# Attention in four whole-pair units, s1 as a row through DRAM, and a new order of a step

## Chip, cores and metric

One core of one Trainium2 chip. The metric is device time in microseconds (us), the median over executions. The kernel before takes 3942.5 us (three runs) and 3941.88 us (3939.61 to 3942.74, four runs) beside the changed one.

## The reference

Two layers over 32 batches of 512 tokens with 512 features, all in 32-bit floats:

```
h  = relu(layernorm(x))
q, k, v = h@Wq + bq, h@Wk + bk, h@Wv + bv                # 8 heads of 64
attn = softmax(q k^T / 8 + (1 - adj) * -1e9)
x  = x + (attn @ v) @ Wo + bo
h  = relu(layernorm(x));   g = h@W
s1, s2 = g@a1, g@a2                                      # one number per token
e  = leaky_relu(s1[:, None] + s2[None, :], 0.2) * adj
x  = x + elu(softmax(e) @ g + beta * g)
```

## The kernel before

It is software-pipelined by hand: step b does V (the v product) and the attention of batch b, the graph part (diagonal, gathers, finals) of b-2, the out projection W of b-1, and the transposes, K and Q of b+1. V, W, K and Q are Strassen products in seven parts. The orders of TensorE and VectorE are fixed by the program text; `later(key, wait, cost, fn)` puts VectorE work `wait` us (of a model of time) later, and `need(key)` forces it out. ScalarE and GpSimd are ordered by a scheduler. Cut to what the argument touches:

```python
def values(b, j, st, half):          # half a pair of heads at a time
    ...
def finish(b, j, st):
    for n in range(b - 1, b + 1):
        need(("at", n))              # the masked exps that read the spread of s1 come first
    pd = psum.tile([P, N], F32, name=f"pd_{b}_{j}", tag="pd")
    ...                              # pd = sum of the exps, by TensorE
    nc.vector.reciprocal(rd, pd)

def logits(b, st):
    dg = row_diag(work, s12[:, 0, :], f"s1_{b}")         # VectorE: diagonal of s1
    def rest(k):
        z = wtile([P, N], f"at_{b}_{k}", "at", 4)
        nc.vector.scalar_tensor_tensor(z, st["ps1"], s12[:, 1, k:k+1], adjT[:, k, :], op0=ALU.add, op1=ALU.mult)
        nc.vector.scalar_tensor_tensor(z, z, ALPHA, z, op0=ALU.mult, op1=ALU.max)
        nc.scalar.activation(z, z, AF.Exp)
        ...                                              # GpSimd: as = sum of the four z
    def spread():
        st["ps1"] = row_bcast(psum, dg, f"s1_{b}")       # TensorE: ones x diagonal, into tag "pd"
        for k in range(T):
            later(("at", b), 0.3, 1.35, lambda k=k: rest(k))

def strassen(pieces, n=1, between=None, early=None):     # in step(b)
    for i, _ in enumerate(pieces):
        if i == 0: ...; att(n, ("qz", "s"))              # attention in 8 half units,
        if i == 4 and between: between()                 # also inside a product
```

Names in the traces: `x`, `y` and `qz` with v, w, k or q are the PSUM tiles in which the seven parts of that product are summed, one line for each part. `ps` are the scores, `e` their exps, `es` the sums of `e`, `po` the values and `pd` the softmax sums of a pair of heads. `oT` is `po` after the division; its sums and differences (the combinations) feed the product W. In the graph part `at` are the masked exps, `as` is their sum over the four tiles, `pe` its sum by TensorE (the diagonal, D in the order strings), `pg` are the gathers (G) and `py` the finals (Y). `hn` is the second normalisation, and the dots make s1 and s2 from it. `pn` are the transposes (N), `pbs` is the product that spreads s1, `dgs` its diagonal. A PSUM `tag` is a buffer that tiles of that tag use in turn.

## Time and profile before

| | before |
|---|---|
| span of the profiled run, mean granted clock of TensorE | 3938.1 us, 0.986 |
| V of batch 0 starts | 98.3 us |
| steps 0 and 1 | 81.2 + 101.8 us |
| a steady step (V to V, batches 2 to 31) | 118.18 us |
| from V of batch 31 to the end | 229.7 us |

TensorE is the bound; the prediction shows its lines. Here is the line of the steady steps of the kernel before (from:to, us, then busy time and count of PE, PEld, DVE, ACT and POOL, the granted clock, the DMA share and GB/s). The clock is 1.00: TensorE never slows in these steps.

```profile
281.30:3708.40 3427.10, 3301.40 (x21928) 1565.80 (x21926) 2155.68 (x3296) 1266.53 (x1917) 1962.58 (x1707) 1.00 0.08 27
```

In the tail it does. Behind a wait of 12.82 us pbs takes 1.97 us there and eight score products 3.74, where the prediction's lines of a steady step show 1.08 and 1.99:

```profile
3799.87 1.97 PE L46 MATMUL pbs<-dgs,ones 128*64 128x512 f32 x4 [12.82 <-DVE dgs L123]
3801.78 3.74 PE L446 MATMUL ps<-qT,kT 64*128 64x512 f32 x8
```

### The profile page before, as it was taken

To read this page: it belongs to the slowest core of one execution; us is meant where nothing else is said; L and a number is where in the kernel's file an instruction comes from. 1 tells how busy PE (TensorE), PEld (TensorE's weight loads), DVE (VectorE), ACT (ScalarE), POOL (GpSimd) and SP (SyncE) were. 2 spreads that over 40 slices of the span, in tenths; PEclk is the share of its full clock that TensorE was granted. 3 is DMA by queue.
4 is the path that set the end of the run, shared out by engine and by line. 5 is a ranking of instruction groups with operands and counts; after the bars stand their busy time and mean duration, and the time that the engine had idled before them with its cause. 6 is when DMAs were issued, how large, how long until landed. Compare 5 with 4: busy or idle time off the path is not lost.

```text
span 3938.1 us, 59207 instructions
## 1 busy us (share of the span) xinstructions
PE 3691.0 (94%) x24302; PEld 1752.0 (44%) x24302; DVE 2414.3 (61%) x3712; ACT 1400.7 (36%) x2119; POOL 2192.5 (56%) x1922
## 2 busy tenths in 40 slices
PE   5989999999999999999999999999999999999976
PEld 3444444444444444444444444444444444444422
DVE  4466566666566665566665566665566665566653
ACT  1333333333333333333333333333333333333321
POOL 4555555555655555655555655555655555655552
PEclk7999999999999999999999999999999999999988
DMA  3000000001100011000111000101100100000001
GB/s 105 11 12 33 33 27 7 33 33 33 33 21 13 33 33 33 33 24 10 33 33 33 33 22 12 33 33 33 33 18 16 33 33 33 33 19 15 22 22 33
DMA packets 60373, 111.61 MB, mean 28 GB/s; under 512 B 5632, under 2 KB 9728, under 8 KB 60096
## 3 DMA queue, kind: packets, MB, share of 16 engines
q1 hardware_dynamic: 54848, 101.73, 7.7%
q10 hardware_dynamic: 4880, 5.24, 0.4%
q8 instruction: 192, 3.15, 0.3%
q0 software_dynamic: 368, 0.79, 0.1%
q14 instruction: 85, 0.70, 0.1%
HBM read 74.19 MB, written 33.55 MB: 27 GB/s over the span
## 4 chain that ended last, share of the span: by engine, by line
PE 72%; DVE 14%; POOL 7%; issue 4%; ACT 3%; DMA 1%; POOLq 0%; ACTq 0%; DVEq 0%
PE pg L46 11%; PE ps L446 11%; PE po L471 9%; PE py L46 6%; PE qz_v L46 4%; PE qz_w L46 4%; POOL es L462 3%; PE pd L486 3%; DVE rd L495 3%; PE y_v L46 3%; PE x_v L46 3%; PE x_w L46 3%; PE qz_k L46 3%; DVE e L451 3%; PE qz_q L46 3%
## 5 line engine op out<-in xcount | busy, mean ns | idle before, releaser
L462 POOL TENSOR_TENSOR es<-es,e 128x512 f32<-128x512 f32 x512 | 645.8, 1292 | 622.1 <-ACT e L455 622.1
L451 DVE TENSOR_TENSOR e<-ps,nmT 128x1024 f32<-128x1024 f32 x512 | 604.3, 1217 | 612.1 <-PE ps L446 612.1
L455 ACT ACTIVATE e<-e 128x1024 f32<-128x1024 f32 x512 | 540.5, 1056 | 519.6 <-DVE e L451 505.1
L446 PE MATMUL ps<-qT,kT 64*128 64x512 f32 x2048 | 513.1, 620 | 0.6 <-POOL qT L402 0.6
L462 POOL TENSOR_TENSOR es<-e,e 128x512 f32<-128x512 f32 x256 | 325.9, 1294 | 334.5 <-PE pd L486 212.7
L471 PE MATMUL po<-e,v 128*64 128x512 f32 x2048 | 496.1, 605 | 0.8 <-ACT e L455 0.7
L495 DVE RECIPROCAL rd<-pd 128x512 f32<-128x512 f32 x128 | 429.8, 3358 | 91.3 <-PE pd L486 91.3
L46 PE MATMUL pg<-at,hn 128*64 128x512 f32 x2048 | 452.8, 595 | 9.5 <-DVE dmax L613 7.7
L46 PE MATMUL py<-w,gT 128*64 128x512 f32 x2048 | 450.0, 592 | 0.0
L446 PEld LDWEIGHTS ps<-qT,kT 64*128 64x128 f32 x2048 | 177.5, 187 | 278.6 <-issue 222.3
L46 PEld LDWEIGHTS pg<-at,hn 128*64 128x64 f32 x2048 | 148.3, 138 | 302.4 <-issue 302.1
L46 PEld LDWEIGHTS py<-w,gT 128*64 128x64 f32 x2048 | 147.6, 137 | 291.8 <-issue 291.8
L640 DVE TENSOR_SCALAR y<-y 128x512 f32<-128x512 f32 x128 | 84.1, 657 | 313.7 <-ACT y L639 313.7
L471 PEld LDWEIGHTS po<-e,v 128*64 128x64 f32 x2048 | 124.0, 136 | 342.2 <-issue 338.2
L267 POOL TENSOR_TENSOR rs<-rs,mhalf 128x1 f32<-128x1 f32 x256 | 168.5, 661 | 153.3 <-DVE rs L266 135.8
L643 POOL TENSOR_TENSOR y<-y,x 128x512 f32<-128x512 f32 x128 | 161.8, 1274 | 139.6 <-DVE y L641 139.6
L510 POOL TENSOR_TENSOR x<-x,c_row 128x512 f32<-128x512 f32 x128 | 162.4, 1290 | 131.3 <-DMA x<-in_x_dram 131.0
L486 PE MATMUL pd<-es,ones 128*64 128x512 f32 x512 | 141.8, 604 | 63.5 <-DVE at L575 55.9
L499 POOL TENSOR_TENSOR oT<-oT,rd 128x512 f32<-128x512 f32 x128 | 168.7, 1318 | 52.4 <-DVE rd L495 47.4
L639 ACT ACTIVATE y<-py,rd 128x512 f32<-128x512 f32 x128 | 87.4, 683 | 246.9 <-PE py L46 183.0
L498 ACT ACTIVATE rj<-rd 128x512 bf16<-128x512 f32 x128 | 80.6, 630 | 247.8 <-DVE rd L495 239.1
L626 ACT COPY gT<-pg 128x512 f32<-128x512 f32 x128 | 74.4, 581 | 260.9 <-PE pg L46 260.9
(190 smaller groups left out, 5694.3 us busy)
## 6 DMA issues: line engine op xcount, KB each, us to landing
x<-in_x_dram SPq DMA_DIRECT2D x128, 256.0 KB, 4.7
x<-in_x_dram SPq DMA_DIRECT2D x64, 512.0 KB, 4.0
out_dram<-y SPq DMA_DIRECT2D x128, 256.0 KB, 3.8
adj<-in_adj_dram SPq DMA_DIRECT2D x4, 256.0 KB, 7.6
w<-in_L_gnn_W_dram ACTq DMA_DIRECT2D x1, 1024.0 KB, 7.3
wk<-in_L_gnn_Wk_dram ACTq DMA_DIRECT2D x3, 256.0 KB, 5.0
wq<-in_L_gnn_Wq_dram ACTq DMA_DIRECT2D x3, 256.0 KB, 8.9
wv<-in_L_gnn_Wv_dram ACTq DMA_DIRECT2D x3, 256.0 KB, 6.5
```

Of the source, the lines that this page charges most:

```text
L46: nc.tensor.matmul(out[s : s + HD], lhsT[:, s : s + HD], rhs, start=start, stop=stop, skip_group_check=onto)
L267: nc.gpsimd.tensor_tensor(rstd, rstd, mhalf[:, 0:1], op=ALU.pow)
L446: nc.tensor.matmul(p[:, s, :], st["kT"][j][rows, ts(k, P)], st["qT"][j][rows, :], start=True, stop=True)
L451: nc.vector.tensor_tensor(e, p, nmT[:, k, :].unsqueeze(1).to_broadcast([P, 2, N]), op=ALU.add)
L455: nc.scalar.activation(e, e, AF.Exp)
L462: nc.gpsimd.tensor_tensor(es[:, s, :], one[:, s, :], e[:, s, :], op=ALU.add)
L471: nc.tensor.matmul(po[s * HD : (s + 1) * HD, :], v[k // 2][:, k % 2, (2 * j + s) * HD : (2 * j + s + 1) * HD], e[k][:, s, :], start=k == 0 ...
L486: nc.tensor.matmul(pd[s * HD : (s + 1) * HD, :], ones[:, :HD], st["es"][j][:, s, :], start=True, stop=True)
L495: nc.vector.reciprocal(rd, pd)
L499: nc.gpsimd.tensor_tensor(o, o, rd, op=ALU.mult)
L510: nc.gpsimd.tensor_tensor(r[:, t, :], r[:, t, :], c_row, op=ALU.add)
L643: nc.gpsimd.tensor_tensor(y, y, st["x1"][t // 2][:, t % 2, :], op=ALU.add)
```

## The change

The intent: attention in 4 units of a whole pair of heads between whole products (values and pd of the pair before, then four scores), so that TensorE goes half as often from 128-row products to the 64-row scores and back (a surplus of 0.35 us a visit in the trace before); s1 turned into a row by two DMAs through DRAM, so that pbs and the PSUM buffer shared with pd go; and an order of step, prologue and tail that has fewer waits.

```diff
-    def row_bcast(psum, dg, name): ...      # ones x diagonal on TensorE
+    def as_row(dst, col, name):
+        d = dram.tile([N], F32, name=f"row_{name}", tag="row")
+        nc.sync.dma_start(d.rearrange("(t p) -> p t", p=P), col, allow_slow_non_contiguous=True)
+        nc.sync.dma_start(dst, d.unsqueeze(0).to_broadcast([P, N]))
@@ attention
-    def values(b, j, st, half):
+    def values(b, j, st):                   # four k at once, then pd in the same tiling
-        for n in range(b - 1, b + 1):
-            need(("at", n))
@@ logits
-        dg = row_diag(work, s12[:, 0, :], f"s1_{b}")
+        as_row(row, s12[:, 0, :], f"s1_{b}")
-                later(("at", b), 0.3, 1.35, lambda k=k: rest(k))
+            later(("at", b), 5.0, 1.45, lambda k=k: rest(k))
@@ step                                      # digits are units of attention
+        order = {0: "0V1N2c3rKQ", 1: "0V1N2W3KQ", B - 1: "0VD1G2YW3", B: "0DGWY", B + 1: "DGY",
+        }.get(b, "0VD1G2YN3WKQ")
... (prologue: masks through four PSUM buffers, row constants moved into step 0; more T and oP buffers)
```

More of the change, by code (lines that the diff above doesn't have):

```diff
@@ L119 @@
     flag = ctile([1, 1], "flag", I32)
-    def row_diag(work, col, name):
-        dg = work.tile([P, T, P], F32, name="dg" + name, tag="dg", bufs=1)
-        nc.vector.tensor_tensor(
-            dg, ident.unsqueeze(1).to_broadcast([P, T, P]),
-            col.unsqueeze(2).to_broadcast([P, T, P]), op=ALU.mult,
-        )
-        return dg
-    def row_bcast(psum, dg, name):
-        p = psum.tile([P, N], F32, name="pb" + name, tag="pd")
-        product(nc, p, ones, dg.rearrange("p t n -> p (t n)"), start=True, stop=True)
-        return p
+    dram = ctx.enter_context(tc.tile_pool(name="dram", bufs=2, space=bass.MemoryType.DRAM))
+    def as_row(dst, col, name):
+        d = dram.tile([N], F32, name=f"row_{name}", tag="row")
+        nc.sync.dma_start(d.rearrange("(t p) -> p t", p=P), col, allow_slow_non_contiguous=True)
+        nc.sync.dma_start(dst, d.unsqueeze(0).to_broadcast([P, N]))
     nc.vector.memset(fin, 0.0)
@@ L192, in edges @@
             nc.vector.tensor_reduce(e0[:, t : t + 1], adj_sb[t], axis=AX.X, op=ALU.max)
-        nc.vector.tensor_scalar(e0, e0, 0.0, 1.0, op0=ALU.is_equal, op1=ALU.mult)
-        pe0 = row_bcast(psum, row_diag(work, e0, "e0"), "e0")
-        nc.vector.tensor_scalar(edge8, pe0, -(HD ** -0.5), HD ** -0.5, op0=ALU.mult, op1=ALU.add)
+        nc.vector.tensor_scalar(e0, e0, 0.0, HD ** -0.5, op0=ALU.not_equal, op1=ALU.mult)
+        as_row(edge8, e0, "e0")
     def masks():
-        for k in range(T):
-            p = psum.tile([P, N], F32, name=f"pa_{k}", tag="x")
+        for k, tag in enumerate(("x", "po", "pd", "s")):
+            p = psum.tile([P, N], F32, name=f"pa_{k}", tag=tag)
             for t in range(T):
@@ L202, in masks, with mask, other @@
             nc.scalar.copy(adjT[:, k, :], p)
+        def mask(k):
             m = wtile([P, N], f"m_{k}", "y", 3)
             nc.vector.tensor_scalar(m, edge8, -(HD ** 0.5), 1.0, op0=ALU.mult, op1=ALU.add)
-            nc.vector.tensor_tensor(m, p, m, op=ALU.max)
+            nc.vector.tensor_tensor(m, adjT[:, k, :], m, op=ALU.max)
             nc.vector.tensor_scalar(nmT[:, k, :], m, -NEG, NEG, op0=ALU.mult, op1=ALU.add)
-        for t in range(T):
+        def other(t):
             sq = wtile([P, N], f"sq_{t}", "y", 3)
@@ L213, in masks @@
             )
+        for k in range(T):
+            later("nm", 1.0, 1.9, lambda k=k: mask(k))
+        for t in range(T):
+            later("bad", 1.0, 1.4, lambda t=t: other(t))
     def load_blocks(w, ap, name):
@@ L244, in value_row, with dot @@
         nc.vector.tensor_add(c_row, c_row, p)
+        combine(nc.gpsimd, wo, ao)
     def row_constants():
         wa = wtile([P, 2, C], "wa", "wa", 1)
+        def dot(g, c, ar):
+            scr = wtile([P, D], f"scr_{g}_{c}", "y", 3)
+            nc.vector.tensor_tensor_reduce(
+                scr, w1[:, c, :], ar, 1.0, 0.0,
+                op0=ALU.mult, op1=ALU.add, accum_out=wa[:, g, c : c + 1],
+            )
+            if c == C - 1:
+                as_row((wa1_r, wa2_r)[g], wa[:, g, :], f"wa{g}")
         for g in range(2):
-            ar = wtile([P, D], f"a_{g}", "at", 4)
+            ar = wtile([P, D], f"a_{g}", "s1", 1)
             nc.gpsimd.dma_start(ar, bass.AP(tensor=a.tensor, offset=a.offset + g * D, ap=[[0, P], [1, D]]))
             for c in range(C):
-                scr = wtile([P, D], f"scr_{g}_{c}", "y", 3)
-                nc.vector.tensor_tensor_reduce(
-                    scr, w1[:, c, :], ar, 1.0, 0.0,
-                    op0=ALU.mult, op1=ALU.add, accum_out=wa[:, g, c : c + 1],
-                )
-        for g, dst in ((0, wa1_r), (1, wa2_r)):
-            p = row_bcast(psum, row_diag(work, wa[:, g, :], f"wa{g}"), f"wa{g}")
-            nc.scalar.copy(dst, p)
+                later("wa", 4.0, 0.75, lambda g=g, c=c, ar=ar: dot(g, c, ar))
     def stats(src, t, u, mv, rstd):
@@ L299, in block, with combos @@
         return pairs[i][:, :, ts(j, H)]
-    def combos(b, name, pairs, tag):
+    def combos(b, name, pairs):
         b11, b12, b21, b22 = (block(pairs, k) for k in range(4))
-        t2, t3, t4 = (wtile([P, 2, H], f"{name}{i}_{b}", tag, 3) for i in (2, 3, 4))
+        t2, t3, t4 = (wtile([P, 2, H], f"{name}{i}_{b}", "T", 5) for i in (2, 3, 4))
         nc.gpsimd.tensor_tensor(t3, b22, b12, op=ALU.subtract)
@@ L319, in turned @@
                 nc.tensor.transpose(p[:, ts(t, P)], xs[t][:, ts(c, P)], ident)
+        for c, tag in ((2, "po"), (3, "x")):
+            p = psum.tile([P, N], F32, name=f"pn{c}_{b}", tag=tag)
+            turned(p, c)
+            nc.scalar.activation(h[1][:, c - 2, :], p, AF.Relu)
         p = psum.tile([P, 2, N], F32, name=f"pn0_{b}", tag="s")
@@ L323, in turn @@
             turned(p[:, c, :], c)
-            nc.scalar.activation(h[0][:, c, :], p[:, c, :], AF.Relu)
-        p = psum.tile([P, N], F32, name=f"pn2_{b}", tag="x")
-        turned(p, 2)
-        nc.scalar.activation(h[1][:, 0, :], p, AF.Relu)
-        p = psum.tile([P, 2, N], F32, name=f"pn3_{b}", tag="qz")
-        turned(p[:, 0, :], 3)
-        nc.scalar.activation(h[1][:, 1, :], p[:, 0, :], AF.Relu)
-        pe(2.8)
-        st["hT"] = combos(b, "tT", h, "tT")
+        nc.scalar.activation(h[0], p, AF.Relu)
+        pe(2.4)
+        st["hT"] = combos(b, "tT", h)
     def seven(name, w, B, tokens, one, two):
@@ L406, in proj_k @@
     def proj_k(b, st):
-        kT = st["kT"] = [wtile([P, N], f"kT_{b}_{f}", "kT", 5) for f in range(C)]
+        kT = st["kT"] = [wtile([P, N], f"kT_{b}_{f}", "kT", 4) for f in range(C)]
         def one(i, k, p):
@@ L441, in scores @@
     def scores(b, j, k, st, tag):
-        p = psum.tile([P, 2, N], F32, name=f"ps_{b}_{j}_{k}", tag=tag)
+        if tag == "xy":
+            ps = [psum.tile([P, N], F32, name=f"ps{s}_{b}_{j}_{k}", tag=tag[s]) for s in range(2)]
+        else:
+            p = psum.tile([P, 2, N], F32, name=f"ps_{b}_{j}_{k}", tag=tag)
+            ps = [p[:, s, :] for s in range(2)]
         for s in range(2):
@@ L446, in scores @@
             nc.tensor.matmul(
-                p[:, s, :], st["kT"][j][rows, ts(k, P)], st["qT"][j][rows, :], start=True, stop=True
+                ps[s], st["kT"][j][rows, ts(k, P)], st["qT"][j][rows, :], start=True, stop=True
             )
-        pe(1.25)
+        pe(0.87)
         e = wtile([P, 2, N], f"e_{b}_{j}_{k}", "e", 4)
-        nc.vector.tensor_tensor(
-            e, p, nmT[:, k, :].unsqueeze(1).to_broadcast([P, 2, N]), op=ALU.add
-        )
-        dve(1.14)
+        if tag == "xy":
+            for s in range(2):
+                nc.vector.tensor_tensor(e[:, s, :], ps[s], nmT[:, k, :], op=ALU.add)
+            dve(1.38)
+        else:
+            nc.vector.tensor_tensor(
+                e, p, nmT[:, k, :].unsqueeze(1).to_broadcast([P, 2, N]), op=ALU.add
+            )
+            dve(1.2)
         nc.scalar.activation(e, e, AF.Exp)
@@ L462, in scores @@
                 nc.gpsimd.tensor_tensor(es[:, s, :], one[:, s, :], e[:, s, :], op=ALU.add)
-    def values(b, j, st, half):
-        if half == 0:
-            st["po"] = psum.tile([P, N], F32, name=f"po_{b}_{j}", tag="po")
-        po, e, v = st["po"], st["e"][j], st["v"]
-        for k in (0, 1) if half == 0 else (2, 3):
+    def values(b, j, st):
+        po = st["po"] = psum.tile([P, N], F32, name=f"po_{b}_{j}", tag="po")
+        e, v = st["e"][j], st["v"]
+        for k in range(T):
             for s in range(2):
@@ L475, in values @@
                 )
-        pe(1.72)
-        if half == 1:
-            finish(b, j, st)
-    def finish(b, j, st):
-        for n in range(b - 1, b + 1):
-            need(("at", n))
-        pd = psum.tile([P, N], F32, name=f"pd_{b}_{j}", tag="pd")
+        pd = st["pd"] = psum.tile([P, N], F32, name=f"pd_{b}_{j}", tag="pd")
         for s in range(2):
@@ L488, in finish @@
             )
-        pe(0.86)
+        pe(4.5)
         if j % 2 == 0:
-            st["o"].append(pair(b, "oT", j // 2, "oP", 3))
+            st["o"].append(pair(b, "oT", j // 2, "oP", 4))
+        nc.scalar.copy(st["o"][j // 2][:, j % 2, :], po)
+    def finish(b, j, st):
         o = st["o"][j // 2][:, j % 2, :]
-        nc.scalar.copy(o, st["po"])
         rd = wtile([P, N], f"rd_{b}_{j}", "rd", 1)
-        nc.vector.reciprocal(rd, pd)
+        nc.vector.reciprocal(rd, st["pd"])
         dve(3.3)
@@ L500, in finish, with residual @@
         if j == NP - 1:
-            st["oT"] = combos(b, "uT", st["o"], "uT")
-    def residual(b, st):
+            st["oT"] = combos(b, "uT", st["o"])
+    def residual(b, st, tag="x1", bufs=2):
         st["x1"] = []
         for i in range(2):
-            r = pair(b, "x1", i, "x1", 2)
+            r = pair(b, "x1", i, tag, bufs)
             nc.sync.dma_start(r, x[b, ts(i, H), :].rearrange("(t p) f -> p t f", p=P))
@@ L561, in third @@
             )
+            st["dots"] += 1
+            if st["dots"] == 2 * T:
+                logits(b, st)
         for t in rows:
@@ L566, in logits @@
     def logits(b, st):
-        need(("hn", b))
         s12 = st["s12"]
-        dg = row_diag(work, s12[:, 0, :], f"s1_{b}")
-        dve(0.65)
+        row = wtile([P, N], f"s1_{b}", "s1", 1)
+        as_row(row, s12[:, 0, :], f"s1_{b}")
         def rest(k):
@@ L575, in rest @@
             nc.vector.scalar_tensor_tensor(
-                z, st["ps1"], s12[:, 1, k : k + 1], adjT[:, k, :], op0=ALU.add, op1=ALU.mult
+                z, row, s12[:, 1, k : k + 1], adjT[:, k, :], op0=ALU.add, op1=ALU.mult
             )
@@ L585, in rest @@
                 nc.gpsimd.tensor_tensor(st["as"], st["as"], z, op=ALU.add)
-        def spread():
-            st["ps1"] = row_bcast(psum, dg, f"s1_{b}")
-            pe(0.86)
-            for k in range(T):
-                later(("at", b), 0.3, 1.35, lambda k=k: rest(k))
-        return spread
+        for k in range(T):
+            later(("at", b), 5.0, 1.45, lambda k=k: rest(k))
     def diagonal(b, st):
+        need(("hn", b))
         need(("at", b))
@@ L651, in new_state, with unit @@
             "x": load(b), "e": [[] for _ in range(NP)], "es": {}, "o": [], "at": [], "g": [], "gT": [],
+            "dots": 0,
         }
-    def unit(b, n, tags=("qz", "s")):
+        norm0(b, states[b]["x"])
+    def unit(b, j):
         s = states.get(b)
-        j, second = divmod(n, 2)
-        if s is not None:
-            for k in range(2):
-                scores(b, j, 2 * second + k, s, tags[k])
-        if second:
-            values(b, j, s, 0)
-        elif j:
-            values(b, j - 1, s, 1)
-        elif b - 1 in states:
-            values(b - 1, NP - 1, states[b - 1], 1)
+        done = (b, j - 1) if j else (b - 1, NP - 1)
+        if done[0] in states:
+            values(*done, states[done[0]])
+        if s is not None and j < NP:
+            for k, tag in enumerate(("s", "xy", "qz", "s")):
+                scores(b, j, k, s, tag)
+        if done[0] in states:
+            finish(*done, states[done[0]])
     def step(b):
@@ L674, in step @@
         prev, old = states.get(b - 1), states.get(b - 2)
-        todo = list(range(8)) if cur is not None else [0] if prev is not None else []
-        def att(n=1, tags=("s", "qz")):
-            for _ in range(n):
-                if todo:
-                    unit(b, todo.pop(0), tags)
-        def strassen(pieces, n=1, between=None, early=None):
-            for i, _ in enumerate(pieces):
-                if i == 0:
-                    if early:
-                        early()
-                    att(n, ("qz", "s"))
-                if i == 4 and between:
-                    between()
@@ L691, in step, with run, V, G @@
-        if cur is not None:
-            strassen(proj_v(b, cur), between=old and (lambda: diagonal(b - 2, old)))
-        else:
-            att()
-            if old is not None:
-                diagonal(b - 2, old)
-        if prev is not None:
-            residual(b - 1, prev)
-        att()
-        if old is not None:
+        def run(pieces):
+            for _ in pieces:
+                pass
+        def V():
+            run(proj_v(b, cur))
+        def G():
             for c in range(C):
-                if c == 2:
-                    att()
@@ L704, in step, with Y, turned @@
                 gather(b - 2, c, old)
-            att()
+        def Y():
             for t in range(T):
-                if t == 2:
-                    att()
                 final(b - 2, t, old)
-        elif cur is not None:
-            att()
-        if nxt is not None:
+        def turned():
             turn(b + 1, nxt)
-        if b == 0:
-            att(3)
-        if b == 1:
-            att(1)
-        if prev is not None:
-            strassen(out_proj(b - 1, prev))
-            if b == 1:
-                att(1)
@@ L722, in step, with W @@
-        if b + 2 < B:
-            new_state(b + 2)
-            norm0(b + 2, states[b + 2]["x"])
-        if nxt is not None:
-            strassen(proj_k(b + 1, nxt))
-        spread = logits(b - 1, prev) if prev is not None else None
-        if nxt is not None:
-            strassen(proj_q(b + 1, nxt), early=spread)
-        elif spread:
-            spread()
-        att(8)
-        if b == B:
+            if b + 2 < B:
+                new_state(b + 2)
+        def W():
+            residual(b - 1, prev, *(("e", 4) if b == B else ()))
+            run(out_proj(b - 1, prev))
@@ new lines, in step @@
+        parts = {
+            "V": V, "D": lambda: diagonal(b - 2, old), "G": G, "Y": Y, "N": turned, "W": W,
+            "K": lambda: run(proj_k(b + 1, nxt)), "Q": lambda: run(proj_q(b + 1, nxt)),
+            "c": lambda: value_row(ao), "r": row_constants,
+        }
+        order = {
+            0: "0V1N2c3rKQ", 1: "0V1N2W3KQ", B - 1: "0VD1G2YW3", B: "0DGWY", B + 1: "DGY",
+        }.get(b, "0VD1G2YN3WKQ")
+        for part in order:
+            if part.isdigit():
+                unit(b, int(part))
+            else:
+                parts[part]()
@@ L734, in step @@
+        if b == 0:
+            need("nm")
+            need("bad")
+        if b == B + 1:
             judge()
@@ L767 @@
                 product(nc, p[:, ts(t, P)], ones, ident, start=t == 0, stop=t == T - 1)
-        norm0(0, states[0]["x"])
+        need(("x", 0))
         combine(nc.vector, wk, ak)
@@ L774 @@
             pass
-        if B > 1:
-            new_state(1)
-            norm0(1, states[1]["x"])
+        new_state(1)
         masks()
+        combine(nc.gpsimd, wv, av, VS)
         for _ in proj_q(0, states[0]):
             pass
-        combine(nc.gpsimd, wv, av, VS)
-        value_row(ao)
-        combine(nc.gpsimd, wo, ao)
-        row_constants()
+        need("nm")
         for b in range(B + 2):
```

## The prediction

> **What bounds the kernel now.** I read the page's busy line first, then the waits of TensorE, then TensorE's instructions in order of time over one step, then GpSimd's over the same step.
>
> ```profile
> PE 3691.0 (94%) x24302; PEld 1752.0 (44%) x24302; DVE 2414.3 (61%) x3712; ACT 1400.7 (36%) x2119; POOL 2192.5 (56%) x1922
> PE pbs L46 <- DVE dgs L123: 59.0, 32, 12.8
> PE pd L486 <- DVE at L575: 55.9, 30, 4.4
> PE pn L319 <- ACT hT L324: 23.5, 32, 0.7
> PE qz_q L46 <- DVE qT L398: 12.3, 28, 0.4
> ```
>
> TensorE is the bound, 94% busy. Its waits are short but come once in every step (32 batches, so about 30 equal steps): the spread of s1 (pbs) waits for the diagonal product dgs, and pd waits for the at work that still reads pbs, because both share one PSUM buffer.
>
> ```profile
> 1565.95 1.08 PE L46 MATMUL pbs<-dgs,ones 128*64 128x512 f32 x4 [1.10 <-DVE dgs L123]
> 1579.88 1.95 PE L46 MATMUL qz_q<-tT,wq 128*64 128x256 f32 x16 [0.44 <-DVE qT L398]
> 1581.66 1.90 PE L46 MATMUL x_v<-wv,hT 128*64 128x256 f32 x16
> 1583.49 1.99 PE L446 MATMUL ps<-qT,kT 64*128 64x512 f32 x8
> 1585.40 1.94 PE L471 MATMUL po<-e,v 128*64 128x512 f32 x8
> 1589.12 1.08 PE L486 MATMUL pd<-es,ones 128*64 128x512 f32 x4 [1.78 <-DVE at L575]
> 1646.68 1.53 PE L319 MATMUL pn<-ident,x 128*128 128x128 f32 x12 [0.74 <-ACT hT L324]
> 1648.52 1.95 PE L46 MATMUL x_w<-wo,oT 128*64 128x256 f32 x16 [0.31 <-ACT hT L327]
> 1684.17 1.08 PE L46 MATMUL pbs<-dgs,ones 128*64 128x512 f32 x4 [1.10 <-DVE dgs L123]
> ```
>
> From pbs to pbs a step takes 1684.17 - 1565.95 = 118.22 us, of which 1.10 + 0.44 + 1.78 + 0.74 + 0.31 = 4.37 us is waiting and 1.0 us the pbs product. The starts also show what a change between kinds of product costs. One Strassen product takes 1.727 us from start to start (others of the row: 1570.64, 1572.37, 1574.09), but x_v to ps is 1.83, ps to po 1.91 and po to the next 1.77. In single instructions the surplus is 0.100 us ahead of ps, 0.104 after its first pair, 0.097 ahead of po and 0.051 after its first pair: 0.35 us for one visit, 8 visits a step, 2.8 us.
>
> GpSimd looks half idle, but its work comes in blocks:
>
> ```profile
> 1590.88 2.51 POOL L462 TENSOR_TENSOR es<-e,e 128x512 f32<-128x512 f32 x2
> 1593.34 1.28 POOL L585 TENSOR_TENSOR as<-as,at 128x512 f32<-128x512 f32 x1
> 1594.58 1.28 POOL L499 TENSOR_TENSOR oT<-oT,rd 128x512 f32<-128x512 f32 x1
> 1658.01 4.99 POOL L462 TENSOR_TENSOR es<-es,e 128x512 f32<-128x512 f32 x4
> ```
>
> Each 128x512 sum costs 1.25 us, and 1.35 when it depends on the one before.
>
> [...]a lone 256 KB store landed 2.0 us after its issue, a lone 512 KB load after 3.8.[...]
>
> **The change, part by part**, in a steady step, with those durations and the built program's order on each engine.
>
> 1. *Removed.* The pbs product and dgs (1.0 + 1.10), the wait of pd for at (1.78), of qz_q (0.44; kT and qT are now rewritten only after the last score), of pn and x_w (1.05; four PSUM buffers instead of three). All on TensorE's chain: 6.4 us.
> 2. *Fewer visits.* Values and the sum pd of the pair before now follow straight on a product of the same tiling, then four scores. Four visits instead of eight: 4 x 0.35 = 1.4 us saved.
>
> Unstalled, a step is then: 4 units of 3.44 (values) + 0.86 (pd) + 3.44 (scores) + 0.35 = 32.3; 28 Strassen products of 1.727 = 48.3; 8 gathers and finals of 3.485 = 27.9; transposes 1.95; diagonal sums 0.46. Sum 110.9 us, 7.3 below before.
>
> 3. *Added waits.* Take 0 for the start of a unit on TensorE. Scores begin at 4.4, e on VectorE starts at 5.6, 6.7, 8.0 and 9.1 (1.15 apart, the split one 1.25), reciprocal 10.3 to 13.6; the four exps end at 7.9, 9.1, 10.3 and 11.45; the product after the unit starts at 8.03.
>  - y copy: the product's third part needs x copied to y by ScalarE, which is behind the exps until 11.45 + 0.58 = 12.0, wanted at 11.5. 0.5 us, in V and in W: 1.0.
>  - Diagonal: on GpSimd the order is six es sums (from 9.15 to 16.65), oT (18.0), three combinations (22.0), and only then the last sum of as (23.4). TensorE reaches the diagonal after V at 20.7. Wait 2.8.
>  - K: after the finals GpSimd must take in the residual x1 by DMA (the load is issued only when y is done; 3.8 us each), the T combinations, then es, oT, T4, and only then the power for rs of the batch after next. Unit 3 starts 69.9 us into the step; GpSimd is through with x1 at about 82.3, es 89.8, rs at 93.2. VectorE's order has the x that needs this rs ahead of the last adds of W, which free qz for K: they end at 95.7, wanted at 92.3. Wait 3.5; it would be near 0 if the x1 loads landed 3 us earlier.
>  - s1 through DRAM: the dots end 4 us into Q, two DMAs take about 6 us (estimate, from the 2.0 us store, more for 512 small elements, and a short load), so the row is there at about 10.5; at is ordered after Q's last write, 13. Hidden.
>
>  Sum 7.3. So a step is 110.9 + 7.3 = 118.2 us: the same as before, with the waits moved from pbs and pd to pe and qz_k.
>
> 4. *Prologue.* V of batch 0 starts at 98.26 before. The first qz_k still waits for GpSimd's weights to about 42 (41.6 before). After K, the masks go through four PSUM buffers without the waits (2.2 instead of 8.9 us), Q runs to 70.1, scores wait for the last two masks and end at 76.3; c_row and wa have moved into step 0. V starts at 76.3: 22 us earlier with a unit already done. Steps 0 and 1 took 81.2 + 101.8 us. Now: step 0 is 74.4 of products and units, plus 3.2 where two units stand close and wait for es, plus 6 for c_row behind a reciprocal: 84. Step 1: about 89. Saved here 10.
> 5. *Tail.* From V of batch 31 to the end 229.7 us before; its idle stretches are 12.8 (pbs), 4.4, 7.7, 12.2 and 8.5. Now the gathers of batch 30 start at about 117 instead of 125, the out projection of 31 comes before the finals of 30, so its norm, its dots and its row (some 30 us) hide half under them: about 213. Saved 17.
>
> Total: 76.3 + 84 + 89 + 29 x 118.2 + 213 = 3890 us. Check by the same sum before: 98.3 + 81.2 + 101.8 + 29 x 118.2 + 229.7 = 3939.
>
> **Rivals.**
> - *The steady step really gets 111 to 113 us*: GpSimd's chains end in time. For it: GpSimd is only 56% busy, and the two waits hang on margins of 3 us and on a scheduled order; an author who tuned this will have looked at it. Against: the order is fixed, and each sum is as long as it was. It gives 76 + 170 + 29 x 112 + 210 = 3704. If only K's wait fails to come, 3890 - 29 x 3.5 = 3789.
> - *The row is late.* If the two DMAs take 11 us or more, at stands ahead of e in VectorE's order, e is late, and the fourth score waits for the first one's PSUM: 1 to 2 us a step, 3920 to 3950.
> - *VectorE becomes the bound* in W to Q: dots, statistics and evacuations there take some 25 us of 36. It is a pile-up that delays kT and qT; up to 1 us a step, 3920.
>
> **Range and chances.** Worked sum 3890. The waits I found are the uncertain part: 7.3 us give or take 1.5, times 29, is 44 us; prologue and tail give or take 12. Errors are a little likelier to the fast side, since K's wait vanishes with an earlier load and such a rebuild is unlikely to have been kept for nothing, so I take 3870 and 3795 to 3930. Faster by 2% needs 3863.7, close to the middle: 0.42. Slower by 2% needs 121 us and more a step with nothing won outside: 0.02.
>
> **What would show it.** Right: no pbs; TensorE's waits led by pe on as (about 2.8 us, 30 times), qz_k on VectorE (2 to 4 us, about 28 times), y parts on ScalarE's y copies (0.5 us, 60 times); V of batch 0 at 76; a step of 116 to 119.5 us. Wrong: pe or qz_k without waits (GpSimd's order matters less than I think), scores waiting for e (row late), or a step under 114 or over 120.

## The result

| | before | after |
|---|---|---|
| median | 3941.88 us | 4145.16 us (4139.84 to 4151.06) |
| span of the profiled run, clock | 3938.1 us, 0.986 | 4138.1 us, 0.953 |
| V of batch 0 starts | 98.3 us | 77.2 us |
| steps 0 and 1 | 81.2 + 101.8 us | 96.9 + 93.6 us |
| a steady step | 118.18 us | 124.72 us |
| from V of batch 31 to the end | 229.7 us | 253.6 us |

The ratio is 1.0517 (95% interval 1.0499 to 1.0535): slower by 5.2%, where 3870 and at worst 3930 were predicted. (A ratio is the mean time of one kernel's fast runs over that of the other's of the same rounds, so not quite the ratio of the medians.) The 200 us between the profiled runs are -21.1 up to V of batch 0, +7.5 in steps 0 and 1, 29 x 6.54 = +189.7 in the steady steps and +23.9 in the tail.

First the waits of TensorE in the changed kernel (line of the waiting product, whom it waited for: us in total, times, longest). Neither pbs nor qz_q in every step is left, as intended; three new waits are worth 315.8 us, 78.9 of it outside the steady steps.

```profile
PE pe L46 <- POOL as L594: 134.9, 32, 38.0
PE qz_k L46 <- DVE x L528: 107.5, 28, 4.5
PE ps L454 <- DVE e L464: 73.4, 32, 3.6
PE py L46 <- DVE y L646: 11.3, 30, 0.4
PE y_w L46 <- ACT y_w L360: 7.3, 30, 0.3
```

Second, the busy times of the steady steps again. The clock is 0.97 here, not 1.00, and TensorE's busy time is 59 us more for the same products, although pbs has gone.

```profile
267.70:3884.50 3616.80, 3360.59 (x21810) 1700.41 (x21808) 2108.43 (x3377) 1269.33 (x1885) 1984.57 (x1707) 0.97 0.09 28
```

Third, TensorE in one step (start, duration, product, in brackets the idle time before it and who ended it):

```profile
1609.97 2.91 PE L46 MATMUL qz_k<-hT,wk 128*64 128x256 f32 x16 [3.40 <-DVE x L528]
1612.61 2.72 PE L46 MATMUL y_k<-tT,wk 128*64 128x256 f32 x16
...
1643.90 1.13 PE L454 MATMUL ps<-qT,kT 64*128 64x512 f32 x4 [2.51 <-DVE e L464]
1644.96 3.60 PE L46 MATMUL x_v<-wv,hT 128*64 128x256 f32 x16
...
1661.09 0.69 PE L46 MATMUL pe<-ones,as 128*64 128x64 f32 x16 [2.17 <-POOL as L594]
1661.60 5.30 PE L483 MATMUL po<-e,v 128*64 128x512 f32 x16
```

Read the durations next to the brackets. A Strassen part lasts 1.90 us elsewhere in the step; qz_k and y_k behind a wait last 2.91 and 2.72, x_v behind the next wait 3.60, and po behind the third 5.30 where 3.60 is usual. The clock record of the trace (each stretch with the clock granted in it) shows why: 69 low windows (clock at a half) in the steady steps, 242.3 us in all, in lengths of 3.41 us or twice that; before has none there. Counting, per wait of over 1 us, how often a low window starts between the wait's beginning and 3.5 us after its end gives 23 of 27 for pe (median wait 2.17 us), 26 of 29 for ps (2.31) and 20 of 28 for qz_k (3.85). In before, 57 waits of 1.09 to 1.78 us in the steady steps were followed by none.

So a steady step after is: 8.83 us of waits (256.1 us over 29 steps), the clock, and the unstalled products. The clock's part cannot be read off directly, since a slow product that ends in front of another wait only shortens that wait; the experiments price it.

### The profile page after: what moved, and what is told of

Same layout as the page of the kernel before. It is cut to its first block, busy times and chain, and to the rows that moved or that the text cites. A ratio compares the mean times of both kernels' runs of the same rounds, so it can differ in the third digit from the quotient of the medians.

```text
span 4138.1 us, 59294 instructions
## 1 busy us (share of the span) xinstructions
PE 3735.1 (90%) x24162; PEld 1884.2 (46%) x24162; DVE 2373.7 (57%) x3804; ACT 1404.8 (34%) x2085; POOL 2217.4 (54%) x1922
## 5 line engine op out<-in xcount | busy, mean ns | idle before, releaser
L464 DVE TENSOR_TENSOR e<-ps,nmT 128x1024 f32<-128x1024 f32 x384 | 456.9, 1218 | 751.7 <-PE ps L454 751.7
L475 POOL TENSOR_TENSOR es<-es,e 128x512 f32<-128x512 f32 x512 | 681.4, 1363 | 0.0
L454 PE MATMUL ps<-qT,kT 64*128 64x512 f32 x2048 | 495.0, 618 | 73.5 <-DVE e L464 73.4
L406 POOL TENSOR_TENSOR qT<-qT,edge 128x256 f32<-128x256 f32 x128 | 90.4, 727 | 420.7 <-DVE qT L402 420.5
L483 PEld LDWEIGHTS po<-e,v 128*64 128x64 f32 x2048 | 157.1, 146 | 272.2 <-issue 246.4
L588 ACT ACTIVATE at<-at 128x512 f32<-128x512 f32 x128 | 80.7, 630 | 450.7 <-DVE at L587 450.7
L496 ACT COPY oT<-po 128x512 f32<-128x512 f32 x128 | 74.4, 581 | 429.3 <-PE po L483 429.3
L645 DVE TENSOR_SCALAR y<-y 128x512 f32<-128x512 f32 x128 | 123.5, 965 | 145.2 <-ACT y L644 145.2
L46 PE MATMUL qz_k<-hT,wk 128*64 128x256 f32 x512 | 88.9, 505 | 121.3 <-DVE x L528 107.5
L592 POOL TENSOR_TENSOR as<-at,at 128x512 f32<-128x512 f32 x32 | 56.8, 1774 | 256.6 <-ACT at L588 256.6
```

The source lines that it names most:

```text
L46: nc.tensor.matmul(out[s : s + HD], lhsT[:, s : s + HD], rhs, start=start, stop=stop, skip_group_check=onto)
L406: nc.gpsimd.tensor_tensor(qh, qh, edge8[:, ts(k, H)], op=ALU.mult)
L454: nc.tensor.matmul(ps[s], st["kT"][j][rows, ts(k, P)], st["qT"][j][rows, :], start=True, stop=True)
L464: nc.vector.tensor_tensor(e, p, nmT[:, k, :].unsqueeze(1).to_broadcast([P, 2, N]), op=ALU.add)
L475: nc.gpsimd.tensor_tensor(es[:, s, :], one[:, s, :], e[:, s, :], op=ALU.add)
L483: nc.tensor.matmul(po[s * HD : (s + 1) * HD, :], v[k // 2][:, k % 2, (2 * j + s) * HD : (2 * j + s + 1) * HD], e[k][:, s, :], start=k == 0 ...
```

## The experiments

Eleven of the twelve kernels are taken from the changed one, one from the kernel before. All gave the right result. My theory: TensorE pays for each of the three waits and then for a half clock after it. The rivals: the waits move elsewhere when taken away, one part alone (the DRAM row, or the whole units) is to blame, or the clock falls for a reason other than idling.

### One wait at a time

**s1's row by TensorE again**, the masks left where the change puts them:

```diff
-        as_row(row, s12[:, 0, :], f"s1_{b}")
+        dg = ...                                    # VectorE: ident x s1
+        def spread():
+            product(nc, p, ones, dg, start=True, stop=True)      # p: PSUM tag "pd"
+            nc.scalar.copy(row, p)
+        later(("at", b), 1.5, 0.0, spread)
```

> The changed kernel, but s1 becomes a row as before (diagonal on VectorE, one product with ones into a PSUM buffer, a copy by ScalarE to SBUF) instead of two DMAs through DRAM. Theory A (TensorE pays for waits and then again for a half clock after each): the wait of the fourth score product for e (73 us in the whole run) goes, with it the half-clock windows that follow it, and the tail's two row trips shorten; one product of 1 us a step is added. About 2.5 us less a step and 20 us less in the tail: 4045, between 4020 and 4085. Rival B (the row is hidden, the loss is elsewhere): only the added product shows: 4145 to 4180.

Measured: 4074.44 us, ratio 1.0338. The wait of ps has gone, the step is 123.17 us. What was gained is less than hoped because TensorE now comes earlier to pe and waits there 3.31 us instead of 2.17 (95.9 us against 62.6 in the steady steps). Why the row was late shows in the changed kernel's DMA issues (the last number is the median from issue to landing) and on VectorE:

```profile
s<-row_s SPq DMA_DIRECT2D x32, 256.0 KB, 4.7
row_s<-s SPq DMA_DIRECT2D x32, 2.0 KB, 8.0
```

```profile
1638.46 0.75 DVE L584 SCALAR_TENSOR_TENSOR at<-s,s,adjT 128x512 f32<-128x512 f32 x1 [3.22 <-DMA s<-row_s]
```

The first DMA is issued at 1625.12; the masks start at 1638.46, 13.3 us later, and VectorE stood still for the last 3.22 us of that with e of the scores queued behind it.

**The last sum of as on VectorE:**

```diff
-            elif k > 1:
+            elif k == 2:
                 nc.gpsimd.tensor_tensor(st["as"], st["as"], z, op=ALU.add)
+            elif k == 3:
+                later(("at", b), 1.2, 0.7, lambda: nc.vector.tensor_tensor(st["as"], st["as"], z, op=ALU.add))
```

> The changed kernel, but the last of the three sums that make as is done on VectorE, not behind GpSimd's other work. Theory A: the wait of the diagonal's product pe for GpSimd (134.9 us in the whole run, 2.17 in a steady step, 38 and 31 in the tail) goes to near 0, and the half clock of the product after it (5.30 us where 3.43 is usual) with it: about 3.4 us less a step, 4045, between 4010 and 4080. Rival B: GpSimd's order is set by what stands ahead of it, and the wait moves to the next product (po, or the next step's y): under 1 us a step, 4115 to 4150.

Measured: 4041.08 us, ratio 1.0252, 121.82 a step. pe waits no more in the steady steps; the waits of qz_k (108.9 us) and ps (65.4) are what they were. On GpSimd in the changed kernel, the sum stands where the prediction had it, behind es, the product oT and the combinations:

```profile
1648.68 5.87 POOL L475 TENSOR_TENSOR es<-es,e 128x512 f32<-128x512 f32 x4
1654.50 1.27 POOL L506 TENSOR_TENSOR oT<-oT,rd 128x512 f32<-128x512 f32 x1
...
1659.78 1.26 POOL L594 TENSOR_TENSOR as<-as,at 128x512 f32<-128x512 f32 x1
```

**The normalisation of the batch two ahead 70 us later:**

```diff
-            later(("x", b), 6.0, 1.0, lambda t=t: first(t))
+            later(("x", b), 6.0 if b < 3 else 76.0, 1.0, lambda t=t: first(t))
```

> The changed kernel, but the statistics and normalisation of the batch two ahead are put 70 us of TensorE work later, out of the stretch in which VectorE also owes x of k. Theory A: the wait of qz_k for VectorE (107.5 us in the whole run, 3.84 in a steady step) goes and with it the half clock of qz_k and y_k: about 5 us less a step, 4000, between 3970 and 4040. Rival B (the normalisation only collides with something else, e of the scores or the copies of O): the wait turns up at another line, 4110 to 4160.

Measured: 3999.42 us, ratio 1.0152, 120.09 a step. The wait of qz_k for VectorE is replaced by one of about 1.1 us for a copy of ScalarE (31.6 us in all). The other two waits change places: ps waits 32.8 us for 66.8, pe 94.8 for 62.6. In the changed kernel VectorE had been idle 4.13 us, waiting for GpSimd's rs of this normalisation, with the adds of W behind it:

```profile
1607.35 0.55 DVE L292 TENSOR_SCALAR x<-x,mv,rs 128x512 f32<-128x512 f32 x1 [4.13 <-POOL rs L273]
```

### All three together

> The first three edits together on the changed kernel: s1's row by TensorE, the last sum of as on VectorE, the normalisation 70 us later. Theory A: with the three waits gone, the step is the unstalled 111 us plus 1 us for the row's product and under 1 us of waits for the copies y: about 112.5 a step, total 3755, between 3720 and 3820, that is 4 to 6% faster than the kernel before, and the whole-unit order is sound in itself. Rival B (the fewer visits and whole units cost something of their own): the step stays over 116, total over 3880.

Measured: 3806.93 us (3806.39 to 3808.00), ratio **0.9662** (0.9646 to 0.9678): faster than the kernel before by 3.4%. The three edits alone saved 70.7, 104.1 and 145.7 us, 320.5 in sum; together 338.2. A step is 114.15 us, 10.57 less than in the changed kernel, and the clock is whole again:

```profile
261.30:3571.60 3310.30, 3259.04 (x21926) 1582.88 (x21924) 2245.15 (x3452) 1281.45 (x1914) 1957.00 (x1682) 1.00 0.08 28
```

This step gives the accounts. Its waits are 51.1 us over 29 steps, 1.76 a step, and pbs takes 0.86 (from its start to the next product's), so the unstalled step is 114.15 - 1.76 - 0.86 = 111.5 us. In the changed kernel 124.72 - 8.83 - 111.5 leaves 4.4 us a step for the clock. The record of the clock nearly agrees: 242.3 us of low windows at half speed lose at most 121, that is 4.2 us a step; the other 0.2 has no explanation. By the same account an unstalled step of the kernel before is 118.18 - 4.33 (waits) - 0.86 (pbs) = 113.0 us, 1.5 more than here, where 1.4 was predicted for the fewer visits; no run isolates that.

### The part with the row in the kernel before

Here s1 goes through DRAM in the kernel before; its half units and its order stay (only the diagonal, which now comes later, stands after V and not inside it).

```diff
-        dg = row_diag(work, s12[:, 0, :], f"s1_{b}")
+        nc.sync.dma_start(d.rearrange("(t p) -> p t", p=P), s12[:, 0, :], allow_slow_non_contiguous=True)
+        nc.sync.dma_start(row, d.unsqueeze(0).to_broadcast([P, N]))
-                later(("at", b), 0.3, 1.35, lambda k=k: rest(k))
+                later(("at", b), 13.0, 1.45, lambda k=k: rest(k))
```

> The kernel before with one part of the change alone: s1 as a row through DRAM in place of the diagonal and its product (pbs). Theory A: pbs and its wait, and the wait of pd for the PSUM buffer that it shares, go (3.9 us a step), but the masks come 13 us after s1 and pe waits behind GpSimd: 0 to 4 us a step back and some half-clock windows, total 3850 to 3960. Rival B (the row costs nothing where there is slack): 114 a step, total under 3850.

Measured: 3984.08 us, ratio 1.0113, 119.39 a step: the mechanism is theory A's, at more than its price (3850 to 3960). pbs and the waits around it have gone; two waits come instead, and behind the second the clock:

```profile
1600.91 1.95 PE L46 MATMUL qz_v<-wv,tT 128*64 128x256 f32 x16 [1.54 <-DVE v L438]
1605.11 1.12 PE L46 MATMUL pe<-ones,as 128*64 128x64 f32 x16 [2.25 <-POOL as L587]
```

Out go 0.86 (pbs), 1.08, 1.78 and 0.38 (the waits of pbs, pd and, nearly all of it, qz_q), 4.1 us; in come 1.57, 2.25 and 25 low windows of together 85.3 us, or 1.5 a step: 5.3 us. 118.18 - 4.1 + 5.3 = 119.4.

### Can the row be hidden?

**The edits for as and the normalisation alone, the row through DRAM** as in the change (the kernel of the three edits with the first one undone).

> The second and third edits only (last sum of as on VectorE, normalisation 70 us later): s1's row goes through DRAM as in the change, the masks called for 5 us after s1 as there. It prices the row through DRAM in an otherwise unstalled step. Theory A (the row comes 13 us after s1, some 2 us too late for the masks, which stop VectorE ahead of e): the product of 1 us is saved, the fourth score product waits 1 to 1.5 us: 113.8 to 115.2 a step against 114.15, and the tail's two row trips cost about 15 us more: 3800 to 3850. Rival B (the row was most of the loss): over 117 a step, over 3900.

Measured: 3856.59 us, ratio 0.9787, 115.29 a step, a little over the range of theory A in both numbers. The fourth score waits 40.5 us over 29 steps (1.4 each), the saved product is 0.86; the tail is 249.4 us against 233.3. So in an otherwise unstalled kernel the row through DRAM costs 49.7 us more than the product that it saves.

**The row through DRAM and the masks moved behind it** (the last two batches by TensorE):

```diff
+        if b < B - 2:
+            as_row(row, s12[:, 0, :], f"s1_{b}")
+        else:
             ...                                          # as in the three edits
-            later(("at", b), 5.0, 1.45, lambda k=k: rest(k))
+            later(("at", b), 13.0 if b < B - 2 else 5.0, 1.45, lambda k=k: rest(k))
```

> The three edits, but s1's row goes through DRAM again (in the last two batches by TensorE) and the masks at are called for 13 us after s1, not 5, so that VectorE does not stop at them ahead of e. Theory A (the row costs nothing if what needs it stands late enough): the product pbs is saved, 1 us a step, and no wait for e appears; at most 1 us of a wait of pe comes back: 113.0 to 114.2 a step against 114.15, total 3770 to 3810. Rival B (the row's 13 us cannot be hidden, pe then waits for the sum as and clocks drop): 115 to 117 a step, 3830 to 3890.

Measured: 4128.67 us, ratio 1.0479, 125.04 a step. That is rival B's side and beyond its range. The masks stand behind e and the reciprocal now, and there their operations take up to 2.4 times as long. First VectorE in this kernel, then in the kernel of the three edits:

```profile
1764.02 1.32 DVE L599 SCALAR_TENSOR_TENSOR at<-s,s,adjT 128x512 f32<-128x512 f32 x1
1765.37 1.65 DVE L602 SCALAR_TENSOR_TENSOR at<-at 128x512 f32<-128x512 f32 x1
```

```profile
1624.03 0.74 DVE L596 SCALAR_TENSOR_TENSOR at<-s,s,adjT 128x512 f32<-128x512 f32 x1
1624.81 0.69 DVE L599 SCALAR_TENSOR_TENSOR at<-at 128x512 f32<-128x512 f32 x1
```

At 1764 GpSimd sums es without a pause (1759.81 to 1768.15), and oT and the combinations follow; at 1624 it is idle. Beside GpSimd's sums 0.69 became 1.65 and 0.74 became 1.76 (in the kernel of the three edits the fourth mask also stands beside es, and takes 1.26 and 1.65), while the reciprocal, which reads pd in PSUM, takes 3.35 us beside the sums es in both kernels. No run shows what in these operations makes the difference. The sum as is so late that pe waits 7.51 us in every step (217.9 us), and every one of these 29 waits was followed by a low window, up to 10.24 us long. The row's 13 us were hidden; the place that this left for the masks was the wrong one.

### The clock by itself

**Filling the waits.** Useless products in front of qz_k (three) and pe (two) of the changed kernel:

```diff
+    def filler(name, n):
+        p = psum.tile([P, N], F32, name=f"fill_{name}", tag="po")
+        for i in range(n):
+            product(nc, p, ones, edge8, start=True, stop=True)
```

> The changed kernel with useless products set into two of the waits: three of 512 columns before qz_k and two before pe, nothing else moved. Theory A (the half clock comes from the idle time itself): the waits shrink by what fills them and the products behind them run at the full clock, about 2.5 us less a step in net: 4070, between 4045 and 4105, and the granted clock rises from 0.953 to about 0.97. Rival B (the clock is lowered for another reason[...]): the products behind the waits stay slow, the clock stays at 0.953, and the time is 4140 to 4200.

Measured: 4198.81 us, ratio 1.0648. The clock did what theory A said (0.972, 105.8 us of low windows in the steady steps for 242.3), the time did what rival B said. TensorE in one step:

```profile
1632.09 1.95 PE L46 MATMUL qz_k<-hT,wk 128*64 128x256 f32 x16 [1.14 <-DVE x L536]
1633.84 1.93 PE L46 MATMUL y_k<-tT,wk 128*64 128x256 f32 x16
...
1640.53 3.63 PE L46 MATMUL qz_k<-tT,wk 128*64 128x256 f32 x16 [3.04 <-ACT qz_k L377]
```

qz_k and y_k run at full speed (1.95 and 1.93 for 2.91 and 2.72), but two parts later there is a new wait of 3.04 us, with its own low window. ScalarE is scheduled, and with the filler in the program the scheduler set hn, which waits for VectorE, ahead of the copy of q_k. So this run cannot tell what the clock costs.

**A pause of one length, idle or busy.** To keep the order of the other engines, both of these add the same chain to the kernel of the three edits, in the middle of the gathers; the busy one has three products in the gap. I compared their instruction orders: ScalarE, GpSimd and VectorE are identical.

```diff
+        product(nc, p, ones, ident[:, :HD], start=True, stop=True)         # pa
+        ...                                     # four small VectorE operations, p -> t1
+        for i in range(3):                      # busy only
+            product(nc, f, ones, edge8, start=True, stop=True)
+        product(nc, p, ones, t1[:, :HD], start=True, stop=True)            # pb waits for t1
```

> A measurement of the half clock by itself, on the kernel of the three edits, which has no low window in its steady steps: in each step, between the second and third product of pg, a tiny product, four small operations of VectorE on its result, and a tiny product that waits for them. TensorE is idle for an estimated 2.5 to 3.5 us there. Theory A (idle TensorE loses its clock): low windows of 3.41 us appear in most steps and the step grows by the pause plus about 1.3 us: 118 to 119.5 a step, total 3925 to 3980. Rival B (the clock falls for other reasons): the step grows by the pause alone and the clock stays at 0.984.

> The same pause as in the idle one, the same instructions in the same order on VectorE, ScalarE and GpSimd, but three useless products of 512 columns (2.7 us) stand in it. Theory A: the pause costs what it lasts and no low windows appear, so although TensorE does more work the whole is 25 to 50 us faster than with the idle pause: 3890 to 3940. Rival B: it is as slow as the idle one or slower by what of the three products does not fit into the pause.

Measured: idle 4001.82 us (ratio 1.0160, clock 0.969, 120.41 a step), busy 3947.01 us (ratio 1.0016, clock 0.984, 118.64 a step). Both are above their ranges; TensorE's wait came out at 3.7 us, over the estimate of 2.5 to 3.5. First TensorE with the idle pause, then with the busy one:

```profile
1616.63 0.48 PE L46 MATMUL pb<-pz,ones 128*64 128x64 f32 x4 [3.71 <-DVE pz L641]
1616.86 9.96 PE L46 MATMUL pg<-at,hn 128*64 128x512 f32 x32
```

```profile
1716.99 2.75 PE L46 MATMUL fill<-edge,ones 128*64 128x512 f32 x12
1720.89 0.34 PE L46 MATMUL pb<-pz,ones 128*64 128x64 f32 x4 [1.16 <-DVE pz L641]
1721.03 7.07 PE L46 MATMUL pg<-at,hn 128*64 128x512 f32 x32
```

The gathers behind the pause take 9.96 us against 7.07; that is a long one, and in the median of the steps, from their start to the next product's, it is 8.57 against 6.87. Low windows follow all 29 idle pauses and none of the 29 busy ones. TensorE does 2.6 us more work a step in the busy kernel and the whole is 54.8 us faster. So here an idle pause costs its own length and then, per step, 1.8 us more (120.41 - 118.64).

**How long may it idle?** The idle pause from 1 to 7 operations of 64 columns, in turn by batch:

> The idle pause again, but made of 1 to 7 small operations of VectorE (64 columns each) in turn from batch to batch, so that one run holds seven lengths of pause, an estimated 1.7 to 2.8 us. It asks how long TensorE may idle. So far waits of 1.0 to 1.8 us were never followed by a low window, waits of 2.17 to 2.31 in 74 of 85 cases. Theory A (a length decides): none of the pauses under about 1.9 us is followed by a low window, nearly all over 2.1 are; the steps of the longest ones are 1 to 2 us longer than the pause alone explains. Rival B (in the changed kernel something else set the clock, and pauses under 3 us are harmless[...]): no low windows at any of the seven lengths, and the steps differ by the pause alone.

Measured: 3943.72 us, ratio 1.0014, clock 0.975. My estimate of the lengths was off: the first two in-place operations last some 1.2 us each (1.17 one, 2.39 two), so the waits were 0.33, 1.3 to 1.62, 2.84, 3.08, 3.30, 3.55 and 3.77 us. Of the six of 1.3 to 1.62 us none was followed by a low window; of those around 2.84 us three of five; of all longer ones 17 of 17. Rival B falls. Between 1.62 and 2.84 us this run holds no sample; there stand the 2.17 us of pe in the changed kernel (23 of 27) and the 2.25 us in the kernel before with the row (25 of 29, with another wait of 1.54 us some 4 us ahead). Length alone does not decide it: 2.17 us is followed more often than 2.84, the 3.85 of qz_k in only 20 of 28 cases, and the 2.2 us of ps with the waits filled in only 8 of 29.

The clock records sort these cases. In each run all low windows start on one grid of 3.413 us (to within 8 ns), which does not follow the steps (one of 124.72 us is 36.5 windows), so I counted how long TensorE is idle inside one window of that grid. Over the steady steps of all 14 traces, a window at full clock with less than 1.70 us of idle was followed by a low one in 0 of 13444 cases, with more than 2.05 us in 285 of 285, between the two in 25 of 115 (in the kernels before and after alone: 0 of 615, 64 of 64, 5 of 39). A low window was followed by another in 102 of 102 cases with 0.74 us of idle or more in it, in 4 of 317 with less. So in these traces whether a low window follows a wait of 2 to 4 us goes with how the grid cuts it; of 44 waits over 4.1 us, twice 2.05, all were followed. Several short waits in one window that add up to 2 us did not occur.

### The tail

With the three edits, W of the last batch put ahead of D, and the dots ahead of the last reciprocal:

```diff
-            ... B: "0DGWY", ...
+            ... B: "0WDGY", ...
+            if b == B:
+                need(("hn", B - 2))       # ahead of finish(...)
```

> All three edits, and a new order of the tail: W of the last batch stands before D of the one before it, and the last reciprocal of a unit behind the dots. Theory A (in the tail TensorE waits for chains on VectorE, 16.8, 12.6, 9.8 and 9.9 us, with nothing to do in between): W fills the first two of these waits and the last batch's chain starts some 30 us earlier: tail 195 to 215 instead of 233, total 3770 to 3790. Rival B (the chain of VectorE is as long in either order): 3800 to 3815.

Measured: 3804.85 us against 3806.93 (ratio 0.9662, the same). The tail is 228.2 us instead of 233.3. The two waits of pbs for the dots (16.8 and 12.6 us) turned into one of 7.8, and W got a new one of 13.7 us for GpSimd's combination of oT, probably because the reciprocal on which that hangs came later: rival B, my mechanism did not carry.

## Why the prediction was wrong

- **Removed waits: right.** pbs, the waits of pd and pn and that of qz_q in every step are gone. But their five terms add up to 5.4 us, not to the 6.4 that the prediction writes; its total does not use that figure.
- **The unstalled step: right.** Predicted 110.9 us, 111.5 by the accounts of the three edits. The whole units are sound: with pbs put back and the three waits taken out or cut to about 1 us, a step takes 114.15 us against 118.18.
- **Added waits: of the three large ones, two found.** pe was worked out as 2.8 and is 2.2 us a step (3.3 where ps does not wait ahead of it, so the nearness is partly luck); qz_k as 3.5 and is 3.7; the copies y as 1.0 and are 0.3 (and py 0.4, not foreseen). Their causes were those named.
- **"The row is there at about 10.5 ... Hidden": failed.** Two DMAs were estimated at 6 us; it is 13.3 from the first issue to the first mask, since the write of 512 single elements alone takes 8.0 (median of 32; 544 packets of under 512 bytes in the 22 us around one). This was the second rival, "11 us or more ... the fourth score waits", whose mechanism came true with 2.3 us a step where 1 to 2 were given. The trace before had a sign of it: its three 2 KB loads of 512 single elements, on GpSimd's queue, landed after 6.3 us, and the estimate took a lone store's 2.0 us where the median of the stores is 3.8.
- **"Sum 7.3. So a step is 110.9 + 7.3": the step that failed.** It charged a wait with its own length. In the steady steps before that was true: the longest wait there was 1.78 us, and the clock 1.00. Waits of 2.2 to 3.9 us cost about 4.2 us a step more through the clock, some 121 us in all, the largest single miss. The products of double length behind the 12.82 us wait in the tail before were a sign of it, and the prediction has no term for them.
- The steady step is thus 0.6 (unstalled) + 1.5 (waits 8.83 for 7.3) + 4.4 (the clock, with the 0.2 left unexplained) = 6.5 us over the prediction, 29 x 6.52 = 189 of the 248 us between the worked sum 3890 and the span 4138.1.
- **V of batch 0: right** (76.3 predicted, 77.2).
- **Steps 0 and 1: failed by 17.5 us** (84 + 89 predicted, 96.9 + 93.6). In step 0 and 1 pc and qz_q wait 6.6 and 6.0 us once each, of which only the first was counted, and the clock of step 0 is 0.91. I did not test this part.
- **Tail: failed by 41 us** (213 predicted, 253.6). The row was to "hide half under" the finals. In the trace pe waits 37.95 and 30.94 us there; of the first, 12.28 us are VectorE waiting for the row, the rest its chain of statistics and dots behind a reciprocal. With the row by TensorE the tail is 237.3 us.
- **The chance** of 0.02 for slower knew the late row as 1 to 2 us a step at most, and the dear wait not at all. The two work together: the late row made a wait of about 2.3 us in every step, and 26 of those 29 waits were followed by a half clock.

```profile
4019.34 1.12 PE L46 MATMUL pe<-ones,as 128*64 128x64 f32 x16 [37.95 <-POOL as L594]
```

## What to carry to other kernels

Where TensorE is the bound, look at the durations of the products behind a wait and at the granted clock: here a wait of over 2 us could cost more than two of 1 us that stand apart. Of the 84 waits of over 1 us for pe, ps and qz_k in the changed kernel (medians 2.17 to 3.85 us), 69 were followed by a low window, of the 57 of 1.09 to 1.78 us in the kernel before none. For a wait with over 2.05 us of idle in one of the 3.41 us windows (285 of 285 were followed) I would take its length plus 1.7 us, an estimate: half of the next 3.41 us is lost at half speed. The idle pause cost 1.8 us a step more than the busy one. Before judging a restructuring by its total, take its waits out one by one; here three small edits, one of which undid the row through DRAM, turned a loss of 5.2% into a gain of 3.4% with the whole units kept. When work is moved to fill a gap on VectorE, see what GpSimd does at that time: the same operation took 0.69 us, or 1.65 beside GpSimd's sums es.
